# A state-space scan with packed-weight work beside it: bit extractions, residual adds and rank products are placed anew, and a broadcast is ordered first

## The chip, the cores and the metric

The kernel runs on one core of a Trainium2 chip. The metric is the device time of that core in microseconds (us). The median of three runs of the kernel before is 998.22 us (997.73 to 998.55).

## What is computed

Two layers, each of an attention-like block and a feed-forward block, each block with a layer norm before it and one after it, and a residual add. The change touches the first block, a Mamba state-space layer, and the weight preparation for the second, a feed-forward layer whose 4-bit weights are packed eight to a 32-bit word. Cut to what matters:

```
x, gate = split(norm(h) @ W_in.T)            # h: (2, 512, 512), D_IN = 1024 channels
x   = silu(conv4(x) + conv_b)
ts, Bm, Cm = split(x @ W_x.T, [32, 16, 16])  # each normed: v * rsqrt(mean(v*v) + 1e-6)
dt  = softplus(ts @ W_dt.T + b_dt)
state = state * exp(dt * A) + (dt * x) * Bm  # per channel, 16 states, scan over 512 steps
y   = sum(state * Cm) + x * D
h   = h + norm((y * silu(gate)) @ W_out.T)

q = (words >> 4*j) & 15                      # j = 0..7, one of eight nibbles
W = q * scale - (zero + 1) * scale           # weights of the feed-forward layer
h = h + norm(swiglu(norm(h) @ W_gate, norm(h) @ W_up) @ W_down)
```

## The kernel before

**Stages.** Rows of h lie on the 128 partitions, four tiles of 128 rows for each of the two batches. Stage 1 (to about 63 us) norms batch 0, projects it to u (8 tiles of 128 channels), forms the ranks ts, B and C, norms them in `ranks_norm`, and writes B and C to a small DRAM tile `scr` (L511). `states` (L515) loads them back as broadcasts: for each of 8 pairs of states a 512 KB tile B and a 512 KB tile C, ordered on SyncE's DMA queue as B0, C0, B1, C1, ... Behind them stands `load_x(1)`, the four tiles of batch 1.

**Scan stage** (stage 2). There are 2 batches x 8 channel tiles x 8 pairs of states = 128 steps `s`. A step is a chain through four engines: ScalarE takes two exponentials into PSUM (`exps`, L960), VectorE multiplies du (PSUM) by B (`times_B`, L976) and scans in place (`scan`, L980), GpSimd multiplies by C in place (`times_C`, L986), TensorE sums over states with an identity (`sums`, L999).

**What sets the order.** The program is traced in an order written by hand, and `pin` (L383) ties every engine's instructions to it. The loop at L1021 goes through the steps. In each it calls `tick()` twice: once before `times_B(s + 1)` and once between that and `scan(s)`. A tick adds one to `now` and resumes every side job whose time has come; a job is a generator, and `yield n` asks to be resumed n ticks later. Since each step has two ticks, an odd `now` lies between a scan and the next multiply by B, an even one between that multiply and the next scan.

**Side jobs that the change touches.**
- `GateUpWords.steps` (L266) unpacks one nibble of the gate and up weights: `nibble` on VectorE (L224), a cast on ScalarE, subtract and multiply on GpSimd (L278, L279), and a store to DRAM. Eleven nibbles are unpacked in stage 1, thirteen in the scan stage by `words_job` (L942). It first calls `gw.move`, which loads packed words (`qw`, L210), scales and zeros (`zs`, L218) for two column cuts into tiles of the scan stage. All of these loads are on SyncE's queue.
- `ranks_norm(1, ...)` forms batch 1's ranks beside the scan: sums of squares over groups of 16 (`ss`, L482 to L487), a power on GpSimd (L489), two products `nb` (L492, L495).
- `add_normed` (L809) norms a row tile of the block's output and adds it to the residual `x` (L819). Batch 0's four tiles pass through it beside the scan, out of `out_job` (L828), which then calls `norm_one` for the statistics of the new x. Batch 1's four pass through it in stage 3 (L1087).

**Queues.** Each engine executes its instructions in order; so does each DMA queue take its orders. Orders on SyncE's queue use eight semaphores in turn, so an order also waits for the transfer eight places before it.

Of the kernel before, what the change touches and what calls it, by code (L numbers as in the profile page):

```python
# [9 lines left out]
F32 = mybir.dt.float32  # L10
# [3 lines left out]
ALU = mybir.AluOpType  # L14
AX = mybir.AxisListType
# [3 lines left out]
P = 128  # L19
# [4 lines left out]
TB = S // P  # L24
# [5 lines left out]
N_ST = 16  # L30
R_DT = 32
R_B, R_C = 32, 48
N_ROW = R_C + N_ST
# [23 lines left out]
def tile_sandwich(  # L57
# [5 lines left out]
    nc = tc.nc  # L63

    def pool(scope, name, bufs=1, space=None):
        kw = {"space": space} if space is not None else {"reuse_waits": "tile"}
        return scope.enter_context(tc.tile_pool(name=name, bufs=bufs, **kw))
# [3 lines left out]
    stat = pool(ctx, "stat", 4)  # L71
# [77 lines left out]
    def apply(dst, src, rs, nm, i):  # L149
        nc.scalar.activation(  # L150
            dst, src, AF.Identity, bias=nm[:, i : i + 1], scale=rs[:, i : i + 1]
        )

    def xs(b):
        return x[b * TB : (b + 1) * TB]

    def norm_tiles(b, idx, dst, bank, xnew, name, interleaved=False):

        n = len(idx)
        rs, nm = scale_bias(moments([xs(b)[i] for i in idx], name), name, n)  # L160
        for j, i in enumerate(idx):
            xn = xnew(f"xn_{name}_{i}")
            src, dst_ = xs(b)[i], xn
            if interleaved:
                src = src.rearrange("p (r k a) -> p r k a", k=KH, a=2)
                dst_ = xn.rearrange("p (k a r) -> p r k a", k=KH, a=2)
            apply(dst_, src, rs, nm, j)
            tp = bank(f"tp_{name}_{i}").rearrange("p (k t) -> p k t", k=KH)
            for kc in range(KH):
                nc.tensor.transpose(tp[:, kc, :], xn[:, ts(kc, P)], ident)  # L170
            nc.scalar.copy(dst[:, :, ts(i, P)], tp)  # L171

    def normed_T(b, dst, bank, xnew, name, **kw):
        norm_tiles(b, range(TB), dst, bank, xnew, name, **kw)

    wgu_d = dram.tile([P, 2, KH, INTER], F32, tag="wgu", name="wgu_d")
# [44 lines left out]
    def nibble(q, qw, j):  # L223
        nc.vector.tensor_scalar(q, qw, 4 * j, 15, ALU.logical_shift_right, ALU.bitwise_and)  # L224

    class GateUpWords:
# [39 lines left out]
        def steps(self, eng=nc.gpsimd):  # L266
            n0, n1, qw, z, s, q_, w_, j = self.todo.pop(0)
            n, nm = n1 - n0, f"gu{n0}_{j}"
            q = q_(nm)
            nibble(q[:, :n], qw[:, :n], j)  # L270
            yield 2
            w = w_(nm)
            if eng is nc.vector:
                eng.tensor_sub(w[:, :n], q[:, :n], z[:, :n])
            else:
                nc.scalar.copy(w[:, :n], q[:, :n])
                yield 2
                eng.tensor_sub(w[:, :n], w[:, :n], z[:, :n])  # L278
            nc.gpsimd.tensor_mul(w[:, :n], w[:, :n], s[:, :n])  # L279
            hp_ = KH * RG  # L280
            rows = slice(j % 2 * hp_, (j % 2 + 1) * hp_)
            nc.gpsimd.dma_start(
                out=wgu_d[rows, :, j // 2, n0:n1].rearrange("r a n -> (r a) n"), in_=w[:, :n]
            )
            yield 2
# [118 lines left out]
    with ExitStack() as mamba:  # L404
# [15 lines left out]
        def jrow(name):  # L420
            return jp.tile([P, S], F32, tag="j", name=name)
# [54 lines left out]
        def ranks_norm(b, ps):  # L476

            sq = jrow(f"sq{b}")[:, : TB * N_ROW].rearrange("p (i r n) -> p i r n", i=TB, n=N_ST)
            nc.scalar.activation(sq.rearrange("p i r n -> p i (r n)"), ps, AF.Square)
            yield 2  # L480
            ss = stat.tile([P, TB, N_ROW // N_ST], F32, tag="ss", name=f"ss{b}")
            nc.vector.tensor_reduce(ss, sq, AX.X, ALU.add)  # L482

            nc.vector.tensor_add(ss[:, :, 1], ss[:, :, 0], ss[:, :, 1])
            nc.vector.tensor_scalar(ss[:, :, 1], ss[:, :, 1], 0.5, None, ALU.mult)
            r = stat.tile([P, TB, 3], F32, tag="rr", name=f"rr{b}")
            nc.vector.tensor_scalar(r, ss[:, :, 1:], 1.0 / N_ST, 1e-6, ALU.mult, ALU.add)  # L487
            yield 1
            nc.gpsimd.tensor_tensor(r, r, mhalf3, ALU.pow)  # L489
            yield 3  # L490
            nb = jrow(f"nb{b}")[:, : TB * N_ROW].rearrange("p (i r) -> p i r", i=TB)
            nc.vector.tensor_mul(  # L492
                nb[:, :, :R_DT], ps[:, :, :R_DT], r[:, :, 0:1].to_broadcast([P, TB, R_DT])
            )
            nc.vector.tensor_mul(  # L495
                nb[:, :, R_DT:].rearrange("p i (r n) -> p i r n", n=N_ST),
                ps[:, :, R_DT:].rearrange("p i (r n) -> p i r n", n=N_ST),
                r[:, :, 1:3].unsqueeze(3).to_broadcast([P, TB, 2, N_ST]),
            )
            st["nb", b] = nb  # L500
# [37 lines left out]
        gw = GateUpWords()  # L538
        with ExitStack() as p1:
# [27 lines left out]
            zds = zeros(dz, [gate_z, up_z], KH, INTER, "gu")  # L567
# [37 lines left out]
            for gi in range(NGI):  # L605
                last = states(0, gi)
# [10 lines left out]
        with ExitStack() as p2:  # L617
# [11 lines left out]
                das.append(da)  # L629


            jobs, now = [], [0]

            def spawn(gen, lag=0):
                jobs.append([now[0] + lag, gen])
# [173 lines left out]
            def add_normed(b, i, src, o):  # L809

                name = f"mo{b}_{i}"
                mv = moments([src], name)
                yield 1
                rs = rstd(mv, name, 1)
                nm = minus_mean(mv, rs, name, 1, True)
                yield 4
                apply(o, src, rs, nm, 0)
                yield 3
                nc.vector.tensor_add(xs(b)[i], xs(b)[i], o)  # L819

            w_out = W_outT.rearrange("(j k p) h -> j p k h", p=P, k=2)

# [117 lines left out]
                yield from ffn0()  # L940

            def words_job():  # L942
                gw.move(g1_tile, zds)
                for _ in range(len(gw.todo)):
                    yield 4
                    spawn(gw.steps())
                yield 6
                st["words"] = now[0]
# [3 lines left out]
            NS = len(order) * NGI  # L952
# [17 lines left out]
            def times_B(s):  # L970
                k, gi = divmod(s, NGI)
                b, c = order[k]
                if gi == 0:
                    nc.vector.tensor_mul(st["du"], u[b][c], st["du"])
                bx = bxs[s] = bxp.tile([P, NG, S], F32, tag="bx", name=f"bx{b}_{c}_{gi}")
                nc.vector.tensor_mul(bx, st["du"].unsqueeze(1).to_broadcast([P, NG, S]), Bbs[b][gi])  # L976

            def scan(s):
                flat = bxs[s].rearrange("p n t -> p (n t)")
                nc.vector.tensor_tensor_scan(  # L980
                    flat, das[s % 2].rearrange("p n t -> p (n t)"), flat, 0.0, ALU.mult, ALU.add
                )
# [38 lines left out]
            for s in range(NS + 3):  # L1021
                k, gi = divmod(s, NGI)
                free = min(free, MM) + STEP
                if gi == 1 and k + 1 < len(order):
                    dt_due = k + 1
                if gi == 2 and k:
                    fin(k - 1)
                for part in ((1, 0) if gi == 2 else (0, 1)):
                    if part == 0:
                        if 0 <= s - 2 < NS:  # L1030
                            free -= sums(s - 2)
                    else:
                        while free > 0 and s < NS:
                            if dt_due and bank_free():
                                turns.append([f"pv{dt_due}", None])
                                spawn(dt_job(dt_due, dt_in(*order[dt_due])), 3)
                                free -= MM
                                dt_due = None
                            cost = next(pe, None)
                            if cost is None:  # L1040
                                break
                            free -= cost
                tick()
                if gi == 4 and k + 1 < len(order):
                    diag(k + 1)
                if s + 1 < NS:
                    times_B(s + 1)
                    if gi == NGI - 2 and k + 1 < len(order):
                        new_du(k + 1)
                tick()  # L1050
                if s < NS:
                    scan(s)
                    if s + 2 < NS:
                        exps(s + 2)
                    times_C(s)
                    if order[k] == (0, NCH - 1):
                        states(1, gi)
                pin()
# [6 lines left out]
        with ExitStack() as p3:  # L1065
# [18 lines left out]
            for i in range(TB):  # L1084
                o = jrow(f"o1_{i}")
# [6 lines left out]
            for i, m in enumerate(IC):  # L1092
                j, e = divmod(i, 2)
                if not e:
                    w = wst.tile([P, 2, H], F32, tag="w4", name=f"wd0_{j}")
                    n = len(IC[i : i + 2])
# [13 lines left out]
            for t in range(TB):  # L1110
                o = o16p.tile([P, H], F16, tag="o16", name=f"o16_0_{t}")
# [272 lines left out]
```

## Time and profile before

| | us |
|---|---|
| median of three runs | 998.22 |
| the profiled execution | 995.69 |
| its span, first to last instruction | 993.8 |
| VectorE busy in the span | 701.7 (71%) |
| TensorE (PE) busy | 876.3 (88%) |
| ScalarE (ACT) busy | 424.9 (43%) |
| GpSimd (POOL) busy | 468.6 (47%) |
| scans L980, 128 times | 2.276 each |
| multiplies by B L976, 128 times | 1.206 each |
| multiplies by C L986, 128 times | 2.364 each |
| bit extractions L224 in the scan stage, 13 times | 0.309 to 7.304 each |

The profile is one execution. Times inside it count from the start of its span. A line of a time line is: start, duration, engine, line of the code, operation, output<-inputs, shapes, and how many instructions were merged; a bracket at its end says how long the engine had been idle and what ended the wait. SPq is SyncE's DMA queue: a row of it is the ordering of a transfer, and its landing is not shown there. The chain of waits follows back from the last instruction to what released each; a DMA in it lasts from its order to the instruction that it released. "issue" is time in which the engine waited for nothing that the profile shows.

### The profile page before, as it was taken

The numbers are of one execution on the slowest core, as the hardware profiler recorded it, in microseconds if no ns is written. First come the engines' busy times: TensorE is split into PE (matmuls) and PEld (weight loads), VectorE is DVE, ScalarE is ACT, GpSimd is POOL, SyncE is SP. The second block draws the span as 40 slices with busy tenths as digits, with TensorE's granted clock in tenths as the row PEclk, the third lists the DMA queues.
The fourth block names the chain that finished last, engine by engine and source line by source line (L and its number), as shares of the span: only waits on it lengthen the run. The fifth ranks groups of instructions, "written<-read, shape, count | busy, mean of one in ns | idle before, by whom it ended". The sixth has DMA issues, their size and how long they took to land.

```text
span 993.8 us, 7230 instructions
## 1 busy us (share of the span) xinstructions
PE 876.3 (88%) x2216; PEld 393.3 (40%) x2216; DVE 701.7 (71%) x785; ACT 424.9 (43%) x639; POOL 468.6 (47%) x341
## 2 busy tenths in 40 slices
PE   6966867787797999867999999999999998999994
PEld 3532323233253444323344344344544444455442
DVE  3839999999999999999999996551540005715225
ACT  4336465466565675456655641031430003322212
POOL 4546888786686776566776675420000000001002
PEclk9977988989999999999999999999999999999998
DMA  6358110100000574320011003542522131100101
GB/s 194 110 183 348 44 53 15 44 36 28 22 22 21 201 241 163 109 62 0 1 42 43 21 21 91 165 154 78 185 76 64 50 103 62 64 1 32 53 0 42
DMA packets 43608, 80.61 MB, mean 81 GB/s; under 512 B 7822, under 2 KB 20217, under 8 KB 43570
## 3 DMA queue, kind: packets, MB, share of 16 engines
q1 hardware_dynamic: 40786, 72.72, 22.4%
q0 software_dynamic: 2496, 6.92, 1.8%
q10 hardware_dynamic: 288, 0.52, 0.1%
q8 instruction: 17, 0.28, 0.1%
q14 instruction: 21, 0.17, 0.1%
HBM read 68.90 MB, written 11.24 MB: 81 GB/s over the span
## 4 chain that ended last, share of the span: by engine, by line
PE 45%; DVE 29%; issue 12%; POOL 4%; ACT 3%; DMA 1%; SPq 0%; DVEq 0%; POOLq 0%; ACTq 0%
DVE bx L980 8%; DVE bx L976 8%; PE py L999 7%; PE pd L1312 6%; PE pup L1249 5%; PE fo L1102 4%; PE fu L349 3%; PE fo L1165 3%; PE fg L349 3%; PE po L1080 3%; DVE q_gu L224 3%; POOL bx L986 2%; PE fu L910 2%; PE fg L910 2%; DVE u L457 2%
## 5 line engine op out<-in xcount | busy, mean ns | idle before, releaser
L986 POOL TENSOR_TENSOR bx<-bx,C 128x1024 f32<-128x1024 f32 x128 | 302.3, 2364 | 150.4 <-DVE bx L980 141.2
L999 PE MATMUL py<-bx,ident 128*128 128x512 f32 x512 | 254.6, 628 | 52.9 <-POOL bx L986 52.7
L980 DVE TENSOR_TENSOR_SCAN bx<-da,bx 128x1024 f32<-128x1024 f32 x128 | 291.2, 2276 | 0.8 <-ACT da L960 0.8
L960 ACT ACTIVATE da<-dt,A 128x511 f32<-128x511 f32 x256 | 176.7, 691 | 206.7 <-DVE bx L980 199.6
L999 PEld LDWEIGHTS py<-bx,ident 128*128 128x128 f32 x512 | 98.2, 199 | 191.9 <-issue 104.4
L976 DVE TENSOR_TENSOR bx<-du,B 128x1024 f32<-128x1024 f32 x128 | 154.3, 1206 | 10.0 <-DMA B<-scr 7.8
L1178 DVE TENSOR_TENSOR it<-it,fu 128x512 f32<-128x512 f32 (+1 forms) x11 | 7.6, 687 | 72.3 <-PE fu L349 72.3
L1249 PE MATMUL pup<-hT_l,wup 128*128 128x512 f32 x128 | 57.6, 605 | 0.0
L674 PE MATMUL pg<-xT,w_g 128*128 128x512 f32 x120 | 56.6, 605 | 0.0
L363 POOL TENSOR_TENSOR sd<-ve,half 128x4 f16<-128x4 f16 x2 | 2.1, 1044 | 114.3 <-DVE ve L361 114.3
L1312 PE MATMUL pd<-wdn,hid 128*128 128x512 f32 x128 | 55.3, 592 | 0.0
L457 DVE SCALAR_TENSOR_TENSOR u<-px,ch,u 128x511 f32<-128x511 f32 (+2 forms) x48 | 35.7, 744 | 14.7 <-ACT u L450 13.3
L910 PE MATMUL fu<-hT_f,wu 128*128 128x512 f32 (+1 forms) x88 | 40.8, 593 | 1.0 <-DVE it L898 1.0
L127 POOL TENSOR_TENSOR rs_lo<-ve_lo,mhalf 128x1 f32<-128x1 f32 x8 | 5.5, 683 | 76.7 <-DVE ve_lo L125 76.7
L349 PE MATMUL fg<-hT_f,wg 128*128 128x512 f32 (+1 forms) x88 | 40.2, 593 | 0.7 <-ACT hT_f L171 0.7
L910 PE MATMUL fg<-hT_f,wg 128*128 128x512 f32 (+1 forms) x88 | 40.5, 592 | 0.0
L349 PE MATMUL fu<-hT_f,wu 128*128 128x512 f32 (+1 forms) x88 | 39.8, 593 | 0.0
L1165 PE MATMUL fo<-wd,it 128*128 128x512 f32 (+1 forms) x88 | 39.6, 592 | 0.0
L1102 PE MATMUL fo<-wd,it 128*128 128x512 f32 (+1 forms) x88 | 37.9, 592 | 0.0
L1312 PEld LDWEIGHTS pd<-wdn,hid 128*128 128x128 f32 x128 | 24.2, 190 | 30.7 <-issue 30.1
L674 PEld LDWEIGHTS pg<-xT,w_g 128*128 128x128 f32 x120 | 23.5, 197 | 31.1 <-issue 30.1
L1249 PEld LDWEIGHTS pup<-hT_l,wup 128*128 128x128 f32 x128 | 24.2, 192 | 28.7 <-issue 28.7
(224 smaller groups left out, 1156.2 us busy)
## 6 DMA issues: line engine op xcount, KB each, us to landing
wo<-in_W_outT SPq DMA_DIRECT2D x20, 512.0 KB
B<-scr SPq DMA_DIRECT2D x16, 512.0 KB
C<-scr SPq DMA_DIRECT2D x16, 512.0 KB
wg<-wgu_d SPq DMA_DIRECT2D x10, 512.0 KB
wu<-wgu_d SPq DMA_DIRECT2D x10, 512.0 KB
w_x<-in_W_in SPq DMA_DIRECT2D x8, 512.0 KB
wgu_d<-w_gu POOLq DMA_DIRECT2D x16, 256.0 KB, 2.4
w_g<-in_W_in SPq DMA_DIRECT2D x8, 512.0 KB
```

The costliest lines, as they stand in the source:

```text
L349: nc.tensor.matmul(ps[:m], w[:, kc, e * P : e * P + m], hT[:, kc, :], start=(kc == 0), stop=(kc == KH - 1),)
L674: nc.tensor.matmul(ps, w[:, k, ts(e, P)], xT[b][:, k, :], start=(k == 0), stop=(k == KH - 1))
L910: nc.tensor.matmul(ps[:m], wt[j][a][:, kc, e * P : e * P + m], hT[:, kc, :], start=(kc == 0), stop=(kc == KH - 1),)
L960: nc.scalar.activation(das[s % 2][:, i, 1:], st["dt", b, c][:, 1:], AF.Exp, scale=A[:, c, n : n + 1])
L976: nc.vector.tensor_mul(bx, st["du"].unsqueeze(1).to_broadcast([P, NG, S]), Bbs[b][gi])
L980: nc.vector.tensor_tensor_scan(flat, das[s % 2].rearrange("p n t -> p (n t)"), flat, 0.0, ALU.mult, ALU.add)
L986: nc.gpsimd.tensor_mul(bxs[s], bxs[s], Cbs[b][s % NGI])
L999: nc.tensor.matmul(st["y"], ident, bx[:, i, :], start=False, stop=(n == N_ST - 1))
L1102: nc.tensor.matmul(fo[t], its[i][:m, ts(t, P)], w[:m, e], start=(i == 0), stop=(i == len(IC) - 1),)
L1165: nc.tensor.matmul(fo[t], its[i][:m, ts(t, P)], w[:m], start=(i == 0), stop=(i == len(IC) - 1),)
L1249: nc.tensor.matmul(ps, w[:, kc, ts(e, P)], src[kc], start=(kc == 0), stop=(kc == KH - 1))
L1312: nc.tensor.matmul(pd, hid[kc][:, ts(i, P)], wdn[kc], start=(kc == 0), stop=(kc == INT // P - 1),)
```

## The change

It has five parts.

1. `GateUpWords.steps` waits, in the scan stage, until `now` is odd before it issues `nibble`.
2. In `ranks_norm` the sums of squares are taken as two reductions, over all 32 elements of ts and over the 16 of B and of C; the addition and the halving that combined two groups go away, and the scalar operation becomes two. For batch 1 the two products `nb` are issued on GpSimd.
3. In `add_normed` the residual add is issued on GpSimd, one tick earlier.
4. The loads of `gw.move` are ordered behind the last of the broadcasts of B and C.
5. The second multiply by B comes behind the first scan instead of before it.

Compared instruction by instruction, the two programs have the same order on TensorE and ScalarE. On SyncE's queue the six loads of the first column cut (two of words, two of scales, two of zeros) move from around `scr` and in front of B0 to behind the four x tiles of batch 1. On VectorE parts 2, 3 and 5 show.

```diff
+    scans, now = [], [0]
...
             q = q_(nm)
+
+            while scans and now[0] % 2 == 0:
+                yield 1
             nibble(q[:, :n], qw[:, :n], j)
...
-            ss = stat.tile([P, TB, N_ROW // N_ST], F32, tag="ss", name=f"ss{b}")
-            nc.vector.tensor_reduce(ss, sq, AX.X, ALU.add)
-
-            nc.vector.tensor_add(ss[:, :, 1], ss[:, :, 0], ss[:, :, 1])
-            nc.vector.tensor_scalar(ss[:, :, 1], ss[:, :, 1], 0.5, None, ALU.mult)
+            ss = stat.tile([P, TB, 3], F32, tag="ss", name=f"ss{b}")
+            nc.vector.tensor_reduce(
+                ss[:, :, 0], sq[:, :, : R_DT // N_ST].rearrange("p i r n -> p i (r n)"), AX.X, ALU.add
+            )
+            nc.vector.tensor_reduce(ss[:, :, 1:], sq[:, :, R_DT // N_ST :], AX.X, ALU.add)
             r = stat.tile([P, TB, 3], F32, tag="rr", name=f"rr{b}")
-            nc.vector.tensor_scalar(r, ss[:, :, 1:], 1.0 / N_ST, 1e-6, ALU.mult, ALU.add)
+            nc.vector.tensor_scalar(r[:, :, 0], ss[:, :, 0], 1.0 / R_DT, 1e-6, ALU.mult, ALU.add)
+            nc.vector.tensor_scalar(r[:, :, 1:], ss[:, :, 1:], 1.0 / N_ST, 1e-6, ALU.mult, ALU.add)
...
-            nc.vector.tensor_mul(
+            eng = nc.gpsimd if b else nc.vector
+            eng.tensor_mul(
                 nb[:, :, :R_DT], ps[:, :, :R_DT], r[:, :, 0:1].to_broadcast([P, TB, R_DT])
             )
-            nc.vector.tensor_mul(
+            eng.tensor_mul(
...
-            jobs, now = [], [0]
+            jobs = []
+            scans.append(1)
...
                 apply(o, src, rs, nm, 0)
-                yield 3
-                nc.vector.tensor_add(xs(b)[i], xs(b)[i], o)
+                yield 2
+                nc.gpsimd.tensor_add(xs(b)[i], xs(b)[i], o)
+                yield 1
...
             def words_job():
-                gw.move(g1_tile, zds)
+                with tc.issue_after(last.ins):
+                    gw.move(g1_tile, zds)
...
-                if s + 1 < NS:
+                if 0 < s < NS - 1:
                     times_B(s + 1)
...
                 if s < NS:
                     scan(s)
+                    if s == 0:
+                        times_B(1)
```

## The prediction

> **What bounds the kernel now.** I read the slices of the page first, then the chain of waits from 54 to 84 us, then the time lines of SyncE's queue (SPq), VectorE (DVE) and GpSimd (POOL) around each edited line. The slices:
>
> ```profile
> PE   6966867787797999867999999999999998999994
> DVE  3839999999999999999999996551540005715225
> ```
>
> A slice is 24.8 us. VectorE is at 9 from 77 to 606 us, the scan stage (128 scans). TensorE is at 9 only in parts of it: in the window 400 to 456 it is busy 43.2 us of 56 while VectorE is busy 55.4. So a microsecond of VectorE in the scan stage is a microsecond of the kernel, unless TensorE or a transfer is next. After 606 TensorE sets the end. Before 77, the chain says:
>
> ```profile
> 66.09 0.40 SPq L520
> 66.49 0.04 issue
> 66.53 0.43 SPq L520
> 66.96 0.04 issue
> 67.01 9.09 DMA B<-scr
> ```
>
> The first multiply needs the broadcast B0, the first scan also stands behind B1. B1 is ordered at 67.01 and lands at 76.10; the scan starts at 77.26. VectorE waits 7.8 us in all.
>
> The scan stage has a cost that the operation list hides:
>
> ```profile
> 89.40 0.94 DVE L224 TENSOR_SCALAR q_gu<-qw_gu 128x512 int32<-128x512 int32 x1
> 117.07 7.30 DVE L224 TENSOR_SCALAR q_gu<-qw_gu 128x512 int32<-128x512 int32 x1
> 305.01 2.20 DVE L484 TENSOR_TENSOR ss<-ss 128x4 f32<-128x4 f32 x1
> 314.18 0.67 DVE L492 TENSOR_TENSOR nb<-pr,rr 128x128 f32<-128x128 f32 x1
> 314.76 2.42 DVE L495 TENSOR_TENSOR nb<-pr,rr 128x128 f32<-128x128 f32 x1
> 418.69 2.01 DVE L819 TENSOR_TENSOR x<-x,o 128x512 f32<-128x512 f32 x1
> ```
>
> The same bit extraction takes 0.42 us at 109.52 and 7.30 us at 117.07; four sums per partition take 2.20. GpSimd explains it:
>
> ```profile
> 304.83 2.36 POOL L986 TENSOR_TENSOR bx<-bx,C 128x1024 f32<-128x1024 f32 x1 [3.76 <-DVE bx L980]
> 314.65 2.39 POOL L986 TENSOR_TENSOR bx<-bx,C 128x1024 f32<-128x1024 f32 x1
> 417.80 2.36 POOL L986 TENSOR_TENSOR bx<-bx,C 128x1024 f32<-128x1024 f32 x1 [1.77 <-DVE bx L980]
> ```
>
> L484 ends at 307.21, when GpSimd ends at 307.19; L495 and L819 likewise. Scans and multiplies by B, with an input in PSUM, are not held.
>
> **Bit extractions: 0.** They cost 27.2 us in the scan stage (13 of them, 0.31 to 7.30), so this edit could be the largest. But in the changed program's instruction order every extraction keeps its place on VectorE: their start lags already put them on odd ticks, between a scan and the next multiply by B. The long ones come behind a batch-norm step (98.48), behind g*=y (117.07), or meet a GpSimd backlog (138.76), and stay so.
>
> **Start: +0.4.** Six word loads leave the front of B0, and the second multiply by B goes behind the first scan. B0 can be ordered once scr has landed. For batch 1, scr was ordered at 324.57 and B at 326.56, so landing takes at most 1.99 us: B0 at 65.2 instead of 66.09 (no earlier than 64.5, when scr's data had moved). That lone batch 1 broadcast had moved its data 3.2 us after its order (3.6 for the W_out load at 623.66), so B0 lands at 68.4 (67.7 to 68.8), not 73.64. The first scan would then end at 71.9, the multiplies by B1 and B2 at 74.6, and the scans at 76.8, 80.1 and 83.4: 6.4 us ahead of before.
>
> Behind the fourth scan stands the first extraction, and its words are now last in the same queue: 16 broadcasts, four x tiles, then the words. SyncE's time line gives the pace, because an order waits for the transfer eight places before:
>
> ```profile
> 76.11 0.32 SPq L520 DMA_DIRECT2D B<-scr  x1
> 77.36 0.32 SPq L520 DMA_DIRECT2D C<-scr  x1
> 78.64 0.32 SPq L520 DMA_DIRECT2D B<-scr  x1
> ```
>
> That is 1.245 us per 512 KB, 421 GB/s, and they land in order. The words follow B0 by 15 broadcasts (18.7 us), four x (2.5) and two 128 KB loads (0.6): 68.4 + 21.9 = 90.3. VectorE, which works in order, waits 6.9 us; behind it are the multiply by B5 and all later scans, and for these GpSimd, TensorE and the exponentials. The extraction then meets an idle GpSimd (0.42), and the multiply by B5 starts at 90.65 instead of 90.25: +0.4 (-0.3 to +1.2 with the bounds above). The Trainium skill (SBUF — State Buffer, "Summary: rules for kernel authors") gives about 358 GB/s for transfers between HBM and SBUF. By it the 9.7 MB need 27.1 us instead of 23.0, which makes this part about +4.5 and the whole -3.6 (an estimate). I take the row: 414 GB/s held from 72 to 92, x included. The scale and zero rows, 4 slow loads, took to 72.4 in front of B; behind the words they should land by 96 and GpSimd first needs them at 100. x lands ahead of the words. W_in's loads stand behind all of these on SyncE's queue; in front of them are the same transfers as before, so they are ordered at about 94 as before (94.35) and TensorE needs the first at 109. None of these costs anything.
>
> **Ranks: -2.9.** Batch 0: four small operations (0.42 + 3 x 0.17) become four (a reduce of half the elements, about 0.28, twice, and two of 0.17): 0. Batch 1: the two products leave VectorE (314.18 to the next multiply at 317.11: 2.9) and cost GpSimd two times about 0.43, from L279's 0.85 for 352 and 1.15 for 512 elements. They come behind the multiply by C ending at 317.04, so nb is ready at 317.9 instead of 317.1. Waiting behind them are the next multiply by C (0.4 late, two steps ahead of its use) and the transposes, which TensorE reached at 318.92. No cost.
>
> The sums of squares no longer have the addition that was held 2.20 us. But scalar operations of 128x4 now come where it stood. The nearest row, L125 (128x1), takes 0.15 at 423.74 amid a GpSimd multiply: by it the change saves 2.0 more. The Trainium skill (SBUF — State Buffer, "Who interferes with whom") says that scalar operations with their operand in SBUF can take a two-port mode and then wait for GpSimd like the two-input addition. By it the wait only moves, and saves 0. I take 0: the extractions are such operations and are held here, and L125 is one element wide.
>
> **Residual adds: -5.2.** Four in the scan stage held VectorE from 400.81, 418.69, 440.52 and 448.98 to its next instruction for 1.94, 1.93, 1.93 and 0.58: 6.4. GpSimd gains 4 x 1.27 (L652, same shape); it is busy 35 of 56 us there. The add comes one tick earlier; ScalarE's apply in front of it had ended at 399.4, 416.8, 438.4 and 443.4, early enough. But it queues behind a multiply by C: at the second, that ends at 420.16, the add at 421.4, but VectorE wants the sum for its statistics at 420.9, so it waits 0.55. The third loses 0.6, the first and fourth have slack. 6.4 - 1.15 = 5.2. What is late next is TensorE, which idles 12.8 us in this window, so the gain passes. The skill (Perfetto Trace Analysis, "Optimizing Scalar/DVE Operations") warns that moving work between these two might not help, since they share a port: by it 0 here and -2.5 in all. The row says otherwise, since two thirds of each long add is waiting, and no other held operation stands near. Batch 1's four adds go to GpSimd under the fo matmuls (654.96 to 692.73; the adds on VectorE began at 660.01, and 4 x 1.27 on GpSimd with its roots between them end by about 670): 0, with some 20 us of cover; without it they cost 4 x 0.6.
>
> **Sum.** +0.4 - 2.9 - 5.2 = -7.7. The profiled execution took 995.69 (span 993.8), which would become 988.0; the median is 998.22, 2.5 above it, and becomes 990.5. A measurement tells 0.2%, 2 us, from no change.
>
> **Rivals.**
> - *The early start is kept* (words land by 83.4): for it, small loads have landed in 2.3 us; against it, the even pace. The start is then -6.4 instead of +0.4, in all -6.4 - 2.9 - 5.2 = -14.5: 983.7. Chance 0.12.
> - *The 128x4 operations are not held*: 988.5. Chance 0.15.
> - *TensorE takes over* behind the ranks (its chain from 323 to 343) and the adds wait longer: about half of the 8.1 passes, and 998.2 + 0.4 - 4.0 = 994.6. Chance 0.12.
> - *Slower: the queue is slow.* From 67 to 72 it moved only 1.22 MB, 244 GB/s. If that comes from the broadcasts' start and not from the scale rows, and lasts, 9.7 MB from 66.2 take 40 us, the first extraction waits to 106, and the start costs 16: 1006.2. It decides once the words land after 98.0, below 305 GB/s. Against it: 414 GB/s once the rows were gone. Chance 0.05.
> - As summed above: 990.5, own range 988 to 993. Chance 0.56.
>
> That the first edit does nothing is part of every case. The range of 983.5 to 995 holds all but the slow queue and the edges. Faster: all of the first two, 0.10 of the third and 0.51 of the last, 0.88. Within 0.2%: 0.02 and 0.04 of these two, 0.06. Slower: the slow queue and 0.01, 0.06.
>
> **What would show it.** A VectorE wait of about 7 us for the words' transfer in front of the first extraction, with the first scan at 69.6; the long extractions unchanged; no adds on VectorE before 606, and GpSimd's of 1.27; two waits of half a microsecond for them; a 128x4 scalar operation of 2 us near 305. I am wrong if extraction 1 doesn't wait, or if the later extractions change length.

## The result and the profile after

The changed kernel takes 990.96 us in the median of five runs (990.72 to 993.87); the kernel before took 997.73 in five runs beside them (994.66 to 998.55). The medians differ by 6.8 us. The ratio, which is taken over all runs and not from the two medians, is 0.9943, with a 95% interval of 0.9922 to 0.9965: 5.7 us, or 0.6%, faster (3.5 to 7.8). Forecast were 990.5 and -7.7. The profiled execution took 990.91 (span 988.8), 5.0 less in the span than the profiled one of before.

The slices of the page, to be laid beside those of before:

```profile
PE   6967766888799999978999999999999998999994
...
DVE  3856999999998999999999996342530014725225
```

VectorE has work earlier in the third slice (49 to 74 us: 5 where it was 3), then a slice of 6, in which it waits. What it waits for is told by VectorE's time line (columns as before; the bracket is the idle time and what ended it):

```profile
70.62 2.29 DVE L990 TENSOR_TENSOR_SCAN bx<-da,bx 128x1024 f32<-128x1024 f32 x1
...
91.77 0.43 DVE L226 TENSOR_SCALAR q_gu<-qw_gu 128x512 int32<-128x512 int32 x1 [6.97 <-DMA qw_gu<-in_up_q]
92.11 1.22 DVE L986 TENSOR_TENSOR bx<-du,B 128x1024 f32<-128x1024 f32 x1
...
118.94 7.30 DVE L226 TENSOR_SCALAR q_gu<-qw_gu 128x512 int32<-128x512 int32 x1
```

The first scan starts at 70.62 instead of 77.26, and the first extraction then stands 6.97 us for its words. The multiply by B5 begins at 92.11, where it began at 90.25: the head start is more than eaten. The extraction that took 7.30 us still takes 7.30. In SyncE's time line the words' orders stand where the forecast saw them, behind 16 broadcasts and four tiles of x:

```profile
64.74 0.33 SPq L527 DMA_DIRECT2D B<-scr  x1
...
84.79 0.55 SPq L212 DMA_DIRECT2D qw_gu<-in_gate_q  x1
86.04 0.50 SPq L212 DMA_DIRECT2D qw_gu<-in_up_q  x1
```

Further on in VectorE's time line stand the new scalar operation of the ranks, and the statistics that wait for GpSimd's residual add:

```profile
307.48 2.25 DVE L492 TENSOR_SCALAR rr<-ss 128x4 f32<-128x4 f32 x1
...
418.61 0.69 DVE L119 BATCH_NORM_STATS2 st_f<-x 128x6 f32<-128x512 f32 x1 [0.45 <-POOL x L827]
```

**Where the time went.** One reads it by following the same instruction through both time lines. The multiply by B5 comes 1.86 us later, and all that follows keeps this distance to 212 us: no extraction changed. Up to the multiply g*=y at 303.17 (300.65 before) it grows to 2.52, because VectorE waits there for TensorE's sum 2.76 instead of 2.11. Behind the sums of squares the distance is 2.19, behind the missing products -0.75 (-0.84 at the first residual add), behind the four residual adds -6.23, and W_out's first matmul begins at 620.85 instead of 627.42: -6.57. So it stays up to the router's matmuls (plg), which begin at 900.57 instead of 907.14. Then 1.7 us are lost, in TensorE's time line of after:

```profile
900.57 4.12 PE L1246 MATMUL plg<-wgt,hT_l 128*128 128x8 f32 x32
904.54 10.00 PE L1261 MATMUL pfe<-hT_l,wfe 128*128 128x512 f32 x16
```

and of before:

```profile
907.14 3.68 PE L1234 MATMUL plg<-wgt,hT_l 128*128 128x8 f32 x32
910.67 8.77 PE L1249 MATMUL pfe<-hT_l,wfe 128*128 128x512 f32 x16
```

The same 48 matmuls (32 plg, 16 pfe) take 13.8 us where they took 12.1. TensorE is busy throughout in both; the granted clock was 0.80 from 898 to 915 in after and 0.89 from 905 to 920 in before. This goes with the execution and not with the change: of the versions below that hold all parts of the change, five took 12.1 for them and two 13.8, and the kernel with the ranks alone took 13.8. What lowers the clock there is not shown.

### The profile page after: what moved, and what is told of

It is laid out like the page before. It is cut to its first block, busy times and chain, and to the rows that moved or that the text cites. A ratio compares the mean times of both kernels' runs of the same rounds, so it can differ in the third digit from the quotient of the medians.

```text
span 988.8 us, 7221 instructions
## 1 busy us (share of the span) xinstructions
PE 880.6 (89%) x2216; PEld 394.3 (40%) x2216; DVE 689.8 (70%) x775; ACT 424.8 (43%) x639; POOL 477.9 (48%) x351
## 3 DMA queue, kind: packets, MB, share of 16 engines
q1 hardware_dynamic: 40786, 72.72, 22.3%
## 4 chain that ended last, share of the span: by engine, by line
PE 43%; DVE 29%; issue 13%; POOL 4%; ACT 3%; DMA 3%; SPq 0%; DVEq 0%; POOLq 0%; ACTq 0%
DVE bx L986 9%; DVE bx L990 8%; PE pd L1324 6%; PE py L1009 5%; PE pup L1261 5%; PE fo L1114 4%; PE fu L354 3%; PE fo L1177 3%; PE fg L354 3%; PE po L1092 3%; DVE q_gu L226 3%; PE fu L919 2%; POOL bx L996 2%; DMA C<-scr 2%; PE fg L919 2%
## 5 line engine op out<-in xcount | busy, mean ns | idle before, releaser
L1009 PE MATMUL py<-bx,ident 128*128 128x512 f32 x512 | 260.7, 641 | 52.7 <-POOL bx L996 52.4
L226 DVE TENSOR_SCALAR q_gu<-qw_gu 128x512 int32<-128x512 int32 (+1 forms) x24 | 33.0, 1376 | 7.0 <-DMA qw_gu<-in_up_q 7.0
```

The source lines that it names most:

```text
L1009: nc.tensor.matmul(st["y"], ident, bx[:, i, :], start=False, stop=(n == N_ST - 1))
```

## The experiments

Times are compared by the ratio to the kernel before, which ran on the same chip in the same session: 999.14 us in its median beside the first four, 998.70 beside the second four, 996.17 beside the last two. A gain in us that follows a ratio is worked out from the ratio, not from the medians.

### One part at a time

**The start alone** (parts 4 and 5), the kernel before with

```diff
-                gw.move(g1_tile, zds)
+                with tc.issue_after(last.ins):
+                    gw.move(g1_tile, zds)
...
-                if s + 1 < NS:
+                if 0 < s < NS - 1:
                     times_B(s + 1)
...
                     scan(s)
+                    if s == 0:
+                        times_B(1)
```

> The kernel before with the changed start alone (loads of the packed words ordered behind the broadcasts, second multiply by B behind the first scan). My theory: the early first scan gains about 6.5 us and the first bit extraction then waits about 7 us for its words, which stand last in SyncE's queue. The multiply by B5 begins at about 92.1 in the time line where it began at 90.25, and the kernel is 1.9 to 2.5 us slower than before. Rival, the early start is kept and other parts lose it later: 6 us faster than before.

Measured: 1002.57 us, ratio 1.0028 (1.0015 to 1.0041), 2.8 us slower (1.5 to 4.1). VectorE's time line has the wait:

```profile
93.62 0.43 DVE L224 TENSOR_SCALAR q_gu<-qw_gu 128x512 int32<-128x512 int32 x1 [7.10 <-DMA qw_gu<-in_up_q]
```

The early start is not kept; alone it costs time. The expected 1.9 to 2.5 lie inside the interval.

**The residual adds alone** (part 3), the kernel before with

```diff
-                yield 3
-                nc.vector.tensor_add(xs(b)[i], xs(b)[i], o)
+                yield 2
+                nc.gpsimd.tensor_add(xs(b)[i], xs(b)[i], o)
+                yield 1
```

> The kernel before with batch 0's and batch 1's residual adds on GpSimd alone. My theory: 5.3 us faster than before, VectorE waiting 0.4 to 0.5 for the sum at the second and the third tile. Rival, that moving work between the two engines brings nothing[...]: no change. Rival, that TensorE takes most of it over as soon as VectorE is early: 2 us faster or less.

Measured: 993.08 us, ratio 0.9943 (0.9925 to 0.9962), 5.7 us faster. VectorE waits 0.45 and 0.44 for the sum at the second and the third tile. Both rivals fall.

**The ranks alone** (part 2 as in the diff of the change).

> The kernel before with the rank part alone (two reductions, two scalar operations, batch 1's two products on GpSimd). My theory: 3.3 us faster than before, of which 2.9 are the products and 0.3 the sums; the scalar operation on 128x4 takes about 2.2 us in place of the held addition. Rival, that what was gained there came from elsewhere: no change.

Measured: 995.61 us, ratio 0.9961 (0.9947 to 0.9975), 3.9 us faster. The scalar operation took 2.26, and the next three multiplies by B stand 3.3 us apart with only scans between them.

By ratio the three make +2.8 - 5.7 - 3.9 = -6.8. The changed kernel's own ratios are -5.7 above and -6.8 in a second measurement below, so the parts add within the intervals. Part 1 alone was not run. In the traces of before and after every extraction of the scan stage has the same neighbours on VectorE, so that the edit has nothing to move.

### Is it the words' place in the queue?

**Words in the middle:** the changed kernel, the two word loads of the first column cut between the fourth and the fifth pair of broadcasts (`words1` orders just these two).

```diff
-            for gi in range(NGI):
+            for gi in range(4):
                 last = states(0, gi)
...
+        with tc.issue_after(last.ins):
+            qw1, last = gw.words1(g1_tile)
+        for gi in range(4, NGI):
+            with tc.issue_after(last.ins):
+                last = states(0, gi)
+        with tc.issue_after(last.ins):
+            load_x(1)
```

> The changed kernel with the two word loads of the first column cut ordered between the fourth and the fifth pair of broadcasts, so the words land at about 79; all else, the scale and zero rows too, stays last. My theory (the words' place in the queue ate the early start): VectorE doesn't wait for words, the multiply by B5 begins at 85.3 instead of 92.1, and the kernel is 6 to 7 us faster than the changed kernel, 12 to 14 faster than before. Rival: the next thing is late, the scale and zero rows at about 95, for which GpSimd waits with the multiplies by C behind it: 2 to 4 us faster than the changed kernel. Rival, the start doesn't matter: as the changed kernel.

Measured: 984.40 us, ratio 0.9858 (0.9832 to 0.9883). The changed kernel was measured a second time beside the next three:

> The changed kernel itself, to stand on the same chip beside the next three. Expected: 0.993 to 0.995 of the time before, as measured first. In the time line the first extraction waits 6.5 to 7.5 us for its words.

Measured: 991.78 us, ratio 0.9932 (0.9908 to 0.9956), the extraction's wait 7.04 us. So the two loads' place is worth 0.0074, or 7.4 us, with some 3.5 us of uncertainty, since the two ratios come from different sessions. The profiles say 6.3: the multiply by B5 begins at 86.61 instead of 92.11, in an execution that ordered scr 0.81 later. VectorE's time line with the words in the middle has no wait left behind the fourth scan:

```profile
83.55 2.28 DVE L1004 TENSOR_TENSOR_SCAN bx<-da,bx 128x1024 f32<-128x1024 f32 x1
85.75 0.94 DVE L226 TENSOR_SCALAR q_gu<-qw_gu 128x512 int32<-128x512 int32 x1
86.61 1.21 DVE L1000 TENSOR_TENSOR bx<-du,B 128x1024 f32<-128x1024 f32 x1
```

The multiply by B5 begins at 86.61 rather than at the expected 85.3: in this execution the first scan came 0.39 later, VectorE waits 1.37 for B2 instead of 0.72, and the extraction is held half a microsecond. The scale and zero rows are not missed.

### What would a place right behind a scan have been worth?

**Extractions as the next instruction after a scan:** the changed kernel, each extraction handed to the loop and issued there (`words_job` also starts a tick earlier).

```diff
-            while scans and now[0] % 2 == 0:
-                yield 1
-            nibble(q[:, :n], qw[:, :n], j)
-            yield 2
+            if scans:
+                pend.append(lambda: nibble(q[:, :n], qw[:, :n], j))
+                yield 3
...
                     scan(s)
+                    while pend:
+                        pend.pop(0)()
```

> The changed kernel with each bit extraction issued as the very next VectorE instruction after a scan; in five places it passes a batch-norm step, a scalar operation or the multiply g*=y, all else has the same order. My theory (the place between scan and next multiply by B isn't enough, an instruction in between lets GpSimd start its multiply and hold the extraction): the extractions that took 2.00, 7.30 and 2.20 us now take about 0.4, 10.4 us less VectorE time by 212, and the kernel is 8 to 10.4 us faster than the changed kernel; those that directly followed a scan and met a GpSimd backlog (5.25, 3.45, 4.02) stay, or shrink if the backlog goes. Rival: TensorE's stream, for which VectorE already waits 2.8 us at 301, takes most of it over: 3 us or less. Rival: GpSimd wins the port in any order: no change.

Measured: 988.84 us, ratio 0.9906 (0.9880 to 0.9933), 2.6 us from the changed kernel's 0.9932, which the intervals don't separate. In the profiles W_out's first matmul begins at 617.37 instead of 621.19; 0.70 of that was there before the first extraction, which leaves 3.1. That is 4.4 less in the extractions, 2.2 more in `ve_n` (below) and 0.8 less of a wait for TensorE at 300. My theory missed by far. The size fits the first rival, but not its cause: VectorE waits less for TensorE at 300, 1.90 instead of 2.71. VectorE's time line says where the gain went:

```profile
109.49 0.40 DVE L226 TENSOR_SCALAR q_gu<-qw_gu 128x512 int32<-128x512 int32 x1
109.81 2.32 DVE L125 TENSOR_SCALAR ve_n<-mv_n 128x4 f32<-128x4 f32 x1
...
118.69 5.80 DVE L226 TENSOR_SCALAR q_gu<-qw_gu 128x512 int32<-128x512 int32 x1
```

with GpSimd's time line beside it:

```profile
109.72 2.38 POOL L998 TENSOR_TENSOR bx<-bx,C 128x1024 f32<-128x1024 f32 x1 [1.00 <-DVE bx L992]
112.21 1.04 POOL L127 TENSOR_TENSOR rs_n<-ve_n,mhalf 128x4 f32<-128x4 f32 x1
```

The extractions that had taken 2.00 and 2.20 fell to 0.40 and 0.32, as expected. But at 109.49 the extraction took a place that had protected another operation: `ve_n` is now second and is held 2.32, until GpSimd's multiply ends at 112.10. In the changed kernel both had passed, `ve_n` first and the extraction behind it, since both start before GpSimd's multiply does:

```profile
111.33 0.14 DVE L125 TENSOR_SCALAR ve_n<-mv_n 128x4 f32<-128x4 f32 x1
111.39 0.42 DVE L226 TENSOR_SCALAR q_gu<-qw_gu 128x512 int32<-128x512 int32 x1
```

```profile
111.56 2.45 POOL L996 TENSOR_TENSOR bx<-bx,C 128x1024 f32<-128x1024 f32 x1 [2.46 <-DVE ve_n L125]
```

So it is not the place that counts but the start: the extractions that start some 0.2 us before GpSimd's next operation are free, those that start while GpSimd is busy, or as late as 0.04 before (118.94 against 118.98 in the changed kernel), are held. At 118.69 GpSimd was in its backlog of two multiplies (4.65 us from 118.43), and the extraction took 5.80 right behind its scan.

**The ranks' scalar operations on GpSimd:**

```diff
-            nc.vector.tensor_scalar(r[:, :, 0], ss[:, :, 0], 1.0 / R_DT, 1e-6, ALU.mult, ALU.add)
+            nc.gpsimd.tensor_scalar(r[:, :, 0], ss[:, :, 0], 1.0 / R_DT, 1e-6, ALU.mult, ALU.add)
```

and the second one likewise.

> The changed kernel with the two scalar operations behind the sums of squares (128x4 and 128x8) on GpSimd, for both batches. My theory (the 128x4 scalar operation is held 2.1 us by GpSimd's multiply by C): batch 1's next multiply by B begins 2.4 us earlier after the sums, and the kernel is 2 to 2.4 us faster than the changed kernel. Rival: TensorE's stream takes it over: no change.

Measured: 987.03 us, ratio 0.9883 (0.9854 to 0.9912). In VectorE's time line the next multiply by B follows the sums of squares at once:

```profile
308.68 0.26 DVE L487 TENSOR_REDUCE ss<-sq 128x4 f32<-128x128 f32 x1
308.86 0.28 DVE L490 TENSOR_REDUCE ss<-sq 128x8 f32<-128x128 f32 x1
309.05 1.22 DVE L986 TENSOR_TENSOR bx<-du,B 128x1024 f32<-128x1024 f32 x1
```

From the first sum to the multiply it takes 0.37 us instead of 2.61 (307.11 to 309.72 in after), so 2.2 come from the edit. By the ratios it is 4.9 us faster than the changed kernel, and the intervals just overlap (0.9908 to 0.9912). The further 2.7 do not come from the edit: from W_out's first matmul to the end this profiled execution took 365.07 us, the changed kernel's 368.01, and TensorE's busy time for the same matmuls was 344.60 against 346.51. In the profiles it is the late clock again: here the 48 matmuls named above took 12.1. For the other runs that is argued; their mean granted clock was 0.961, the changed kernel's 0.957.

**All three edits together.**

> The changed kernel with all three edits: word loads between the fourth and fifth pair of broadcasts, extractions right behind the scan, scalar operations of the ranks on GpSimd. If they add: the 6.6 us of the first, 8 to 10 of the second, 2 of the third, 17 to 19 us faster than the changed kernel, about 973. If TensorE takes over: near the version with the first edit alone, 980 to 984.

Measured: 981.48 us, ratio 0.9826 (0.9802 to 0.9850), 10.6 us from the changed kernel's ratio. W_out's first matmul begins 10.4 earlier. 973 was too much in the main by what the extractions had failed to bring.

### Which kind of operation is held?

The multiplies by B and the scans, with an input in PSUM, are never held. The Trainium skill (VectorE: DVE Perf Modes, "What auto-detection actually checks") gives, beside a condition on the shape, what the two-port mode needs: a single source, and it and the destination in SBUF. Then an extraction with a second input in PSUM should escape. **Mask in PSUM:** the changed kernel with

```diff
+            nc.vector.scalar_tensor_tensor(
+                q, qw, 4 * j, mask[0].to_broadcast(list(q.shape)),
+                ALU.logical_shift_right, ALU.bitwise_and,
+            )
...
-                nc.vector.memset(da[:, :, 0:1], 0.0)
+                nc.vector.memset(da[:, :, 0:1].bitcast(I32), 15)
+                if i == 0:
+                    mask.append(da[:, 0, 0:1].bitcast(I32))
```

> The changed kernel, each bit extraction of the scan stage made an operation with two tensors, the words in SBUF and the mask 15 in PSUM (the column of zeros that starts each scan holds the bit pattern 15, a number of about 2e-44, instead of 0). It keeps its place and the same result. My theory (a one-tensor scalar operation from SBUF to SBUF is what GpSimd holds, an operation with one input in PSUM is not, as the multiplies by B): each extraction takes 0.4 to 0.65 us wherever it stands, the 13 take about 7 us in place of 27, and the kernel is 10 to 18 us faster than the changed kernel, less than 20 because GpSimd is busy 92.6 of the 115 us from 100 to 215 and must follow. Rival: it is held all the same, no change. Rival: TensorE takes it over, 5 us or less.

Measured: 977.30 us, ratio 0.9803 (0.9777 to 0.9830), 0.0129 or 12.9 us below the changed kernel's second ratio; W_out's first matmul begins 12.5 earlier (608.73 instead of 621.19). The group of these extractions in the scan stage (count, busy time, mean ns):

```profile
L227 DVE SCALAR_TENSOR_TENSOR q_gu<-qw_gu,da 128x352 int32<-128x352 int32 (+1 forms) x13 | 7.3, 564 | 7.2 <-DMA qw_gu<-in_up_q 7.2
```

7.3 us in place of 26.7, none above 0.69: the hold is gone wherever the extraction stands, as the theory had it. The edit changes two things, the kind of the operation and where its second input lies, and a mask in SBUF was not run. But the trace of before holds the comparison for another kind, TENSOR_TENSOR of 128x512: the residual add with both inputs in SBUF took up to 2.02 us, the product du<-u,du with one in PSUM 0.70 at most, though 8 of its 16 begin in the middle of a GpSimd operation, as 9 of the 13 masked extractions do. So there it is the input's place that decides. The product L495, held for 2.42 us, has both inputs in SBUF too: `pr` is a copy of the ranks. Of the 19.4 us VectorE gives 5.70 back in one place, in its time line:

```profile
144.06 0.69 DVE L992 TENSOR_TENSOR du<-u,du 128x512 f32<-128x512 f32 x1 [5.70 <-ACT du L986]
```

ScalarE had itself waited for TensorE's gate matmul, and TensorE for GpSimd, in TensorE's time line:

```profile
131.94 3.78 PE L1017 MATMUL py<-bx,ident 128*128 128x512 f32 x4 [4.85 <-POOL bx L1004]
```

GpSimd is busy 89.6 of the 100 us from 100 to 200, VectorE 92.9. At this place it is GpSimd that sets the time.

**Words in the middle, ranks' scalar operations on GpSimd, mask in PSUM**, the edits as above:

> The changed kernel with the word loads between the fourth and fifth pair of broadcasts, the scalar operations of the ranks on GpSimd, and the extractions with the mask in PSUM. If the gains add: 7 + 2 + 10 to 18, about 965 to 973. If GpSimd or TensorE is the next limit: 975 to 981, as the version with the first two and extractions right behind the scan.

Measured: 970.96 us (969.05 to 972.42), ratio 0.9738 (0.9708 to 0.9768). The gains add nearly: 7.4 + 2.2 + 12.9 make 22.5 from the changed kernel, the ratios show 19.4. Up to W_out's first matmul they add fully, which begins at 598.90 instead of 621.19, 22.3 earlier; behind it this profiled execution took 370.03 us and the changed kernel's 368.01. It is the fastest version found, 2.6% faster than the kernel before.

## Why the prediction was right, and where it was off

- **Extractions, 0: right.** Twelve of the thirteen took what they had taken, within 0.1 us; the first took 0.43 instead of 0.94, since GpSimd had run out of work. The edit chooses the side of the step, not the next place, and the extractions were on that side already. The place itself would have brought 3.
- **Start, +0.4: right in mechanism, too small.** It was 1.86 in the profiles and 2.8 (1.5 to 4.1) by itself, outside the bounds of -0.3 to +1.2. Two terms of the sum were mis-sized. B0's first use came at 69.29, 4.5 after its order at 64.74 (4.0 to 4.8 in the nine executions with this start); I had taken 3.2 from a lone broadcast, and here seven more broadcasts were ordered right behind it (that these share the engines with it is argued, not shown). From there to the words' landing it took 22.5 (22.9 with the start alone) instead of 21.9, whose three terms make 21.8. So the fourth scan began 4.7 ahead of before (82.52 instead of 87.20), not 6.4; by the forecast's own rows, 83.4 against 89.40 at its end, it would have been 6.0. The reason that I gave for the sign, the words' place in a queue that lands in order at an even pace, is shown by the 7.4 us that two moved loads bring.
- **The queue's pace: right.** With the skill's 358 GB/s the start would have cost 4.5 (an estimate), with the trace's pace 0.4; 1.86 and 2.8 lie between. The pace itself was the trace's: after shows 413 GB/s from 70 to 90 us. What the sum didn't have is the beginning, 216 GB/s from 66.8 to 70, with no scale rows in front. So the slow moving that the last rival feared does come with the broadcasts' start, but it doesn't last.
- **Ranks, -2.9: right,** 3.27 in the profiles: 2.94 from the products, as forecast, and 0.33 from the sums, which I had put at 0. By itself the part brought 3.9 (2.5 to 5.3).
- **The 128x4 operation held: right.** It took 2.25, and the skill's rule of two-port scalar operations was the better guide than the 0.15 of L125, which is one element wide.
- **Residual adds, -5.2: right,** 5.4 in the profiles, with waits of 0.45 and 0.44 for my 0.55 and 0.6. (The long adds in the prediction's rows do not end with GpSimd's multiply but half a microsecond behind it, 420.70 against 420.16: they run once it has ended.) The skill's warning that work moved between these two engines might not help did not come true here, where most of each long add was waiting for the other engine.
- **Not in the sum:** 0.66 lost to TensorE's sum at 301, whose cause stays open, and 1.7 to the clock at 900, which is an accident of one execution. At W_out's first matmul the profiles show -6.57 against the sum's -7.7: the start's error of 1.46 and the 0.66, less about 1.0 that ranks, adds and the rest of the scan stage brought beyond the forecast.
- **From profile to median.** I added 2.5 because before's profiled execution lay that much below its median; after's lies on its median. In the profiles the gain is 5.0, in the ratio 5.7, in the medians 6.8, and the closeness of 990.5 to 990.96 is in part luck: the runs of single parts put the start 2.4 us dearer than forecast and the adds and the ranks 0.5 and 1.0 better, so that the errors in part cancel.

Of the rivals, the early start that is kept would have needed the words by 83.4; they came at 91.7. (The 2.3 us named for it are those of stores on GpSimd's queue.) TensorE took nothing over behind the ranks: the adds' gain passed whole.

## What to carry to other kernels

A load that is ordered late in a queue for the sake of an earlier one is itself due somewhere; work out when it lands and who stands behind its user, and move only what is not due. Where a short VectorE operation takes as long as GpSimd's current one, change the operation (an input in PSUM, or another engine) rather than its place: the place is good only for what starts before GpSimd's next operation. And an operation that mostly waits for the other engine is worth moving to it.

## What was not expected of the hardware

- Whether a short operation is held is settled at its start. A 128x4 scalar operation took 0.14 us when it started 0.2 us before GpSimd's multiply and 2.32 when it started 0.1 behind it. Scalar operations of one element per partition (128x1) were not held even in the middle of a multiply: 0.15 us at 423.74 in before, where GpSimd is busy from 423.05 to 425.41.
- The 944 matmuls from W_out's first to the end took 365.1 to 371.3 us in twelve profiled executions, whatever the version, with TensorE's busy time at 344.6 to 351.3. That spread is as large as most of the effects here, so that single profiled spans don't rank these kernels. The time lines up to 620 us do better, once the end of stage 1 is taken off: scr was ordered between 62.5 and 64.3 us.
